# The last stage of a four-layer kernel, its operations issued in a listed order in place of a greedy one

## The chip, the core and the metric

The kernel runs on one core of a Trainium2 chip. The metric is the device time of one execution in microseconds (us). Three runs of the kernel before gave 3882.3, 3878.21 and 3872.31 us, so its median is 3878.21 us. The core's engines are called PE (matrix multiply; PEld is its weight load), DVE (vector), ACT (scalar and activation), POOL (GpSimd) and SP (it issues most of the DMA transfers). Each of them works through its own list of instructions, and a semaphore holds an instruction back until what it reads has been written.

## The reference, cut to what matters

The reference takes an image of 4 samples, 56 x 56 pixels, 128 channels, and passes it through four layers, each with a residual: window attention, a graph layer, a Fourier neural operator with attention, and a convolution. The changed code is the last stage: the end of the third layer and the whole of the fourth. This is what it has to compute:

```python
attention = _inorm(projd + xa, norm_g[1], norm_b[1])
an = _inorm(attention, norm_g[2], norm_b[2])
m = _fno_layer(an, wM0, wM0s, bM0s, (H, W), (norm_g[3], norm_b[3]), act=True)
m = _fno_layer(m, wM1, wM1s, bM1s, (H, W), (norm_g[4], norm_b[4]), act=False)
output = _inorm(m, norm_g[5], norm_b[5]) + attention
# ... x = x + output; then the fourth layer on the group norm of x:
y = lax.conv_general_dilated(xc, W, window_strides=(1, 1), padding=[(pad_t, pad_t), (0, 0)], ...) + b
agent_sum = jnp.sum(y, axis=3, keepdims=True)
time_sum = jnp.sum(y, axis=2, keepdims=True)
g = (agent_sum + time_sum - y) / scale
out = jax.nn.relu(g + res)
```

`_fno_layer` is a Fourier transform cut to a few frequencies, a weighting of these, and the transform back, plus a skip connection. In the kernel, transforms are matmuls with constant matrices, and every `_inorm` needs a sum over the whole image before anything after it can go on. The fourth layer needs the group norm's sums over a whole sample.

## The kernel before, where the change and the prediction touch it

The last stage is written as a plan of 788 operations. Each has an engine, a cost in the plan's own model, what it comes after, and which buffers it takes and gives back. The plan is issued by a greedy rule: of all operations that may go, the one that could start first in the model goes next, ties in the order of the plan.

```python
class Plan:
    HOP, SETS = 0.25, 1.3
    # ...
    def issue(self):
        free, table, left = {}, None, list(self.ops)
        # ...
        while left:
            best = None
            for op in left:
                if any(a.end is None for a in op.after):
                    continue
                t = max([free.get(op.engine, 0.0)] + [a.end + a.lag + self.HOP * (a.engine != op.engine)
                                                      for a in op.after])
                # ... buffers that have to come free
                if t is not None and (best is None or t < best[0] - 1e-9):
                    best = t, op
            # ...
            op.run()
            free[op.engine] = op.end = t + op.cost
```

One half of a sample (28 of its 56 rows) goes through `half_sample`. The halves are called 0a, 0b, 1a ... 3b in this document. This is the chain of one half, cut to the operations that come up later; `op(engine, cost, after)` adds an operation, and the work of an operation is on the lines under it.

```python
h = over_h("y", "h", [put_dc], d, v)              # PE  h1: transform along one axis
c = over_c("c", k.gw, [plain], ds, v)             # PE  c1: mix of channels
# ... adds (DVE), squares (ACT)
w1, z1, z = over_w("att", adds)                   # PE  w1, then a copy on ACT
var = sums("s1", k.ones_px, "sq", HH, sqs, [sq])  # PE  s1, then a reduction on DVE
total, square, t1 = weighted(w.M0, [z1], z, y)    # PE  two products, DVE two, POOL total, ACT square
factors = everywhere("r", 2, [inverses], ...)     # PE  F1, then copies on DVE
var = sums("f", k.ones[:112], "t1", 32, [square], [t1])     # PE  f
# POOL skip (2.8), POOL normed (2.8)
h = over_h("y", "h", [total, under], d, v)        # PE  h2
sc = scaled("h", "f", w.g123, [h, inv], d, y)     # DVE
c = over_c("c", k.gv, [sc], ds, v)                # PE  c2, then adds2 (DVE), gelus (ACT)
w2, z2, z = over_w("g", gelus)                    # PE  w2
total, square, t1 = weighted(w.M1, [z2], z, y, "dc")        # PE  p2, ... POOL total, ACT square
var = sums("q", k.ones[:112], "t1", 32, [square], [t1])     # PE  q
h = over_h("y", "h", [total, var], d, v)          # PE  h3
sc = scaled("h", "q", w.ng[:, 4:5], [h, inv], d, y)         # DVE
@op("POOL", 0.9, [sc, spread_copy])
def less_mean():
    nc.gpsimd.tensor_add(V.v[:, :, :HH], V.v[:, :, :HH], bc(V.dcs, 2, HH))
c = over_c("c", k.gv, [less_mean], ds, v)         # PE  c3
for i in range(2):                                # DVE adds3, ACT squares
    # ...
var = sums("r5", k.ones_px, "sq", HH, sqs, [sq])  # PE  r5
factors = everywhere("r5x", 1, [view], ...)       # PE  F5
for i in range(2):
    p = plan.add("POOL", 1.5, last, [factors])
    p = plan.add("POOL", 1.8, sum2, [p, sum1], (), [a] if i else [])
    whole.done.append(plan.add("DVE", 1.1, stats, [p]))
@op("DVE", 1.77, whole.done[-2:])
def sums_a(): ...
@op("DVE", 3.0, whole.done[-2:])
def sums_l(): ...
```

After both halves, `last_layer` does the fourth layer of a sample. Its operations are called L0 to L3 here.

```python
@op("DVE", 0.3, whole.done)
def aggregate(): ...
@op("PE", 0.3, [aggregate], [b1])
def means(): ...
# deviations (DVE), variances (PE), root (ACT), scale (DVE)
@op("PE", 1.5, [variances] + whole.sums, [b3])
def over_l(): ...
# offsets (DVE), over_taps (PE), rows (DVE)
for i, (j, n) in enumerate(pieces):               # four pieces of 16, 16, 16 and 8 rows
    p1 = plan.add("POOL", n / 10, spread, [rows], [o])
    p2 = plan.add("PE", 0.3 * n, convolve, [scale] + whole.done, [d])
    p = plan.add("DVE", 0.06 * n, add, [p1, p2], (), [d])
    p = plan.add("ACT", 0.055 * n, relu, [p])
    plan.add("POOL", 0.115 * n, store, [p], (), [o, ("x", b)], lag=3.0)
```

The stage begins with eight turns (transposes on PE) that bring the attended rows out of a big buffer: four for samples 0 and 1 (`R0`), four for samples 2 and 3 (`R1`). That buffer's place is taken by the residual images `o_x`, whose loads therefore wait for the last turn; `constant` (ACT) and then `sum1` (POOL) are the first to use them.

## Time and profile before

The page of the profile covers one execution of 3873.3 us. The stage in question is its last tenth: the first turn starts at 3471.46 us, the last matmul ends at 3867.2 us.

| part of the span | us |
|---|---|
| whole span | 3873.3 |
| first matmul of the last stage to its last matmul | 395.7 |
| from the last matmul to the end | 6.1 |
| PE busy over the whole span | 3546.0 |
| POOL busy over the whole span | 1210.6 |

How to read what follows: a line of a timeline gives start, duration, engine, line of the kernel, instruction, tiles written and read, and in square brackets how long the engine sat idle before it and what released it. The chain of waits names for each engine and line what it waited for, with the total, the number of times and the longest. The half-sample names are not in the trace; they follow from the order in which the program's instructions stand on each engine, since every engine executes its list in that order.

## The change

The greedy rule is taken out, and `issue` gets a list of all 788 operation numbers. It goes through the list and only asserts that everything an operation comes after has been issued, and that the buffers it takes are free by then. The operations themselves, their buffers and their dependencies are as before. The list was searched for in the plan's model; it is for a shorter stage than the greedy order gives.

```diff
-    HOP, SETS = 0.25, 1.3
...
-    def issue(self):
-        free, table, left = {}, None, list(self.ops)
-        # ... the greedy rule shown above
-        return max(op.end for op in self.ops)
+    def issue(self, order):
+        assert sorted(order) == list(range(len(self.ops)))
+        users, taken = {}, {n: [] for n in self.buffers}
+        for op in self.ops:
+            for g in op.gives:
+                users[g] = users.get(g, 0) + 1
+        for n in order:
+            op = self.ops[n]
+            assert all(a.end for a in op.after)
+            for b, key in op.takes:
+                taken[b].append(key)
+                old = len(taken[b]) - 1 - self.buffers[b]
+                assert old < 0 or not users[b, taken[b][old]]
             op.run()
+            op.end = True
             for g in op.gives:
                 users[g] -= 1
...
+OUTPUT_ORDER = """
+0 40 119 227 306 10 3 2 1 4 5 13 12 11 14 15 6 9 7 8 18 19 16 17 41 228 120 42 307 121 43 45 44 122 124 229 47
+... 19 more lines ...
+781 782 785 786 787
+"""
...
-        plan.issue()
+        plan.issue([int(n) for n in OUTPUT_ORDER.split()])
```

The two orders, engine by engine, at the places that the prediction speaks of (read from the instructions of the two built programs; an apostrophe marks the second of two equal operations of a half):

```
PE, start
 before: R0 turns x4, 0a.h1 0b.h1 0a.c1 1a.h1 1b.h1 0a.w1, R1 turns x4, 0a.s1 0a.p1 0a.p1' 0b.c1 0a.F1 ...
 after:  R0 turns x4, 0a.h1 0b.h1 0a.c1 1a.h1 0a.w1 0b.c1 0a.s1 0a.p1' 0a.p1 0b.w1 0b.s1 0a.F1 0b.p1 0a.f
         0b.F1 0b.p1' 0a.h2 1a.c1 1b.h1 0b.f 0a.c2 1a.s1 0b.h2, R1 turns x4, 0a.w2 0b.c2 0a.p2' 0a.p2 1a.w1 ...
POOL, middle
 before: ... 2a.last 2a.sum2 2a.last' 2a.sum2' 2b.total' 3a.clear' 3a.sum1 3b.clear 2b.less_mean ...
 after:  ... 3a.skip L1.spread x3 3a.normed 3a.clear' 2b.total' 3a.sum1 2a.less_mean 3b.total 2b.less_mean
         3b.skip 3b.normed 3b.sum1 3a.total' 2a.last' 3b.clear' 2b.last' ...
DVE, end of sample 0
 before: ... 0b.stats' 0b.sums_a 0b.sums_l L0.aggregate 2a.add L0.deviations ...
 after:  ... 0b.stats' L0.aggregate 0b.sums_l 0b.sums_a L0.deviations ...
PE, tail
 before: L1.convolve L2.means 3a.q L1.convolve x3 L2.variances L2.over_l 3a.h3 3b.w2 L2.over_taps 3a.c3 3b.p2 3b.p2'
         3a.r5 3a.F5 3b.spread 3b.q 3b.h3 3b.c3 3b.r5 3b.F5 L2.convolve x4 L3.means L3.variances L3.over_l
         L3.convolve L3.over_taps L3.convolve x3
 after:  L1.convolve 3b.c2 3a.q L1.convolve x2 3b.w2 L1.convolve 3b.p2' L2.means 3b.p2 L2.variances L2.over_l
         3a.h3 3b.spread L2.over_taps 3b.q 3a.c3 3b.h3 3a.r5 3b.c3 3a.F5 3b.r5 3b.F5 L2.convolve x3 L3.means
         L2.convolve L3.variances L3.over_l L3.convolve L3.over_taps L3.convolve x3
POOL, tail
 before: 3b.total' 3a.last 3a.sum2 3a.last' 3a.sum2' 3b.less_mean 3b.last ...
 after:  3b.total' 3a.less_mean L2.spread x3 3b.less_mean 3a.last' 3a.last 3a.sum2' 3a.sum2 3b.last' ...
DVE, tail
 before: 3a.stats 3b.scaled 3a.stats' 3a.sums_a 3a.sums_l 3b.adds3 3b.adds3' 3b.reduce ...
 after:  3a.adds3 3a.adds3' 3b.scaled 3a.reduce ... 3b.adds3 3a.copies 3b.adds3' 3b.reduce ... 3a.stats' 3b.copies ...
```

## The prediction

> **What bounds the kernel now.** I read the page first, for where the span goes, and then only the last stage: its timeline on PE, the chain of waits on PE, and the timelines of POOL and DVE just ahead of each long wait. The page says that PE is busy almost everywhere, so an order can only win what PE idles or what it does slowly:

> ```profile
> span 3873.3 us, 79430 instructions
> PE   6899999989998998999989989999998989989988
> PEclk8999999999999999999999999999998989998888
> ```

> Each digit is the share, in tenths, of a slice of 96.8 us. In the last four slices, where the stage lies (3471.5 to 3867.2 us, 395.7 us), PE is at 8 to 9 tenths, and its granted clock is lower than in most of the kernel. The stretches of the stage show both:

> ```profile
> 3471.00:3500.00 29.00, 24.13 (x188) 20.21 (x188) 10.11 (x20) 14.76 (x32) 0.28 (x2) 0.94 0.39 143
> 3540.00:3556.00 16.00, 16.00 (x82) 13.52 (x83) 1.92 (x5) 4.34 (x5) 7.61 (x4) 0.57 0.00 0
> 3600.00:3620.00 20.00, 17.61 (x91) 11.39 (x91) 12.81 (x27) 5.75 (x7) 1.28 (x1) 0.66 0.06 24
> 3727.00:3754.00 27.00, 20.47 (x118) 14.24 (x110) 14.62 (x21) 9.42 (x11) 10.76 (x8) 0.62 0.00 1
> 3804.00:3832.00 28.00, 17.88 (x79) 10.15 (x80) 13.10 (x22) 3.35 (x6) 14.14 (x10) 0.57 0.00 1
> ```

> Columns: stretch, length, busy us of PE, PEld, DVE, ACT, POOL, granted clock, DMA share, GB/s. In the last two PE idles 6.5 and 10.1 us and its clock is about 0.6. What ended the waits, longest first, by the chain of waits on PE:

> ```profile
> PE o_b L1967 <- ACT o_t L1956: 9.1, 4, 6.5
> PE o_d L1900 <- POOL o_v L2159: 6.3, 4, 3.6
> PE o_b L1967 <- ACT o_sq L2019: 3.9, 1, 3.9
> PE o_b L2241 <- DVE o_mv L2236: 2.8, 2, 2.1
> ```

> All waits on PE inside the stage add up to 38.1 us. The cause of the 6.5 us wait (2b.q) is seen on POOL: the total that 2b.q needs (L1952) starts only after two multiplies and two additions of another half (L2182, L2185).

> ```profile
> 3724.23 1.50 POOL L2182 TENSOR_TENSOR o_a<-o_a,o_f 128x784 f32<-128x784 f32 x1
> 3725.81 1.85 POOL L2185 TENSOR_TENSOR o_x<-o_x,o_a 128x784 f32<-128x784 f32 x1
> 3727.63 1.49 POOL L2182 TENSOR_TENSOR o_a<-o_a,o_f 128x784 f32<-128x784 f32 x1
> 3729.20 1.83 POOL L2185 TENSOR_TENSOR o_x<-o_x,o_a 128x784 f32<-128x784 f32 x1
> 3730.99 2.08 POOL L1952 TENSOR_TENSOR o_y<-o_t,o_t 112x896 f32<-112x896 f32 x1
> ```

> In the tail the same happens twice: 3b.less_mean (L2159, 0.84 us) stands behind the last and sum2 of 3a, and on DVE 3b.adds3 (L2166) behind 3a's sums:

> ```profile
> 3813.66 1.77 DVE L2196 TENSOR_REDUCE o_nl<-o_x 128x28 f32<-128x1568 f32 x1
> 3815.34 3.01 DVE L2200 TENSOR_REDUCE o_na<-o_x 128x56 f32<-128x1568 f32 x1
> 3818.26 2.22 DVE L2166 SCALAR_TENSOR_TENSOR o_a<-o_t,t_w_ms,o_d 128x392 f32<-128x392 f32 x4
> ```

> 3b.c3 had ended at 3816.5, so adds3 lost 1.8 us there, and PE stood for 3.91 us.

> [...] half-clock windows begin in or right after the gaps at 3604, 3652, 3727, 3768 and 3807 us, but those at 3652 and 3768 are of 1.4 and 1.7 us only, and the window at 3541 has no gap ahead, only over_w and other matmuls of few columns. So a removed gap is worth more than itself, but not every slow window goes with one.

> **The change part by part.** No operation is added or removed; 737 of the 788 stand at another place in the order of issue. First the sum of the stage. Taking for each kind of PE operation its fastest instance (w 3.09, h 1.57, c 1.44, product 1.5, a 16-row convolve 4.51, and so on, by the count in the plan) gives 286.5 us of PE work. The remaining 109.2 us of the 395.7 are 38.1 of waits, 51.4 lost in half-clock windows (half of PE's busy time in them), and 19.7 of small scatter. The last item stays.

> For the waits I compared, for every pair of PE operations joined through other engines, the PE work placed between them in each order with the shortest time between them that this trace shows. Where the filler is shorter, the rest is a wait.

> Waits that I expect to go:
> - 2b.q: 6.53. In the new order 2b.total' stands ahead of 2a's last and sum2 (6.7 us of POOL).
> - 3b.c3: 3.65, of which some 3.5 go, since less_mean no longer stands behind 3a's four operations and h3 to c3 needs only scaled (1.15) and less_mean (0.84).
> - 3b.r5: 3.91, of which 1.6 go. From c3 to r5 the shortest seen is 3.12, and 0.81 of filler (3a.F5) lies between.
> - means of L0 and what follows, 2.06 + 0.33: aggregate stands ahead of sums_l and sums_a (3.02 + 1.77). Means of L1 and what follows, 0.71 + 0.81 + 0.35: the filler from 1b.F5 to it is 20.4 us instead of 11.3, where 14.2 was the shortest seen.
> - the first product after w2, 1.54 (0a) and 1.05 (1a): no filler before, a c (1.44) now.
> - 3b.c2: 1.73, filler 0 before, 5.4 now.
> - c3 of 0b, 1b and 2a behind less_mean: 1.55 + 0.30 + 0.78.
> - 3a.F5 1.44, L3.variances 1.28, 2a.f 1.42: each has filler now.
> Sum: 6.5 + 3.5 + 1.6 + 2.4 + 1.9 + 2.6 + 1.7 + 2.6 + 4.1 = 26.9 us.

> Waits that the new order makes, by the same comparison: 0a.w1 0.9, 0b.F1 2.1 (s1 to F1 needs 5.06, filler 2.93), 1b.f 1.6, L1.over_taps 1.7, 2a.F1 1.35, 3a.w1 0.9, L2.over_taps 2.5 (needs 4.18, filler 1.69), 3a.r5 1.5. Sum 12.5. Net: 26.9 - 12.5 = 14.4 us less waiting, so about 24 us remain.

> The clock: of the windows lost, I take as gone the ones that the removed gaps set off: 3732 to 3753 (9 us lost), 3603 to 3616 (6.5), 3770 to 3773 (1.7), 17 in all. The tail's window (3807 to 3831, 7.5) I keep, since h3, c3, r5 and F5 of two halves are still alone there. The new waits will set off one or two others at the mean of 4.7 (51.4 over 11): minus 6. Net 11 us. The 6.1 us after the last matmul stay.

> The plain sum is 14.4 + 11 = 25 us. I take off 5 for queues that pairs of operations do not show (below), and predict 3878 - 20 = 3858 us.

> **The rivals.**
> (1) The order is good only in its model: where it has put operations next to each other to the tenth of a us, a real one that is late holds up its whole engine. Against it: the costs in the plan are near the measured ones (sums_l 3.0 and 3.05, last 1.5 and 1.50, skip 2.8 and 2.81), so the model sees the queues of POOL and DVE. For it: it knows nothing of the clock, and its PE times are full-speed ones. This would make about 3875.
> (2) A transfer takes the place: the R1 turns come at about 36 us of PE work instead of 14, so the residual images are loaded some 20 us later. Before, all three loads were issued at 3496.4 to 3497.7 and moved until 3510; constant began at 3512.0. Now constant stands on ACT only about 4.2 us after the last R1 turn (w2 3.1, its copy 0.9). If the first image lands alone, in a third of the 13 us, ACT waits 1 us and PE nothing. If all three land together, ACT waits 9 us and 1a's products some 4.6 us more. For the first: the loads are issued one after another on one queue. This would make 3863.
> (3) The clock gives all back: the same slow windows elsewhere, and only 14 us of waits gone: 3868. Or it gives more: with half of the 51 us gone, 3842.

> **Range and chances.** Rival 3 both ways spans 3842 to 3868, rival 1 adds up to 3875, and the three runs before differ by 10 us. So 3858, with 3838 to 3875 for 8 in 10. A change of 2% is 77.6 us, of the 109 that are not work at its fastest; 89.5 of those are waits and clock, so faster by more than 2% would need nearly all of them: 0.02. Slower by more than 2% would need three times the waits there are now: 0.01. Within 2%: 0.97.

> **What would show it right or wrong.** Right: no q waits over 2 us for its square on ACT; c3 no longer waits 3.6 us for POOL; the waits on PE in the stage sum to 20 to 28 us; the mean clock in the stage rises from 0.85 (the twelve stretches of the stage, weighted) to near 0.88; the stage's first to last matmul takes 370 to 380 us. Wrong: the waits sum to over 35, or ACT stands on the load of o_x for over 5 us, or the clock stays. The first 3471 us must be unchanged; if they move by more than 5 us, the comparison itself is blurred.

## The result and the profile after

The kernel with the listed order takes 3816.0 us (median of four runs; 3815.0 to 3821.9) against 3878.4 us before (four runs; 3872.3 to 3882.3): a ratio of 0.9844, with a 95% interval of 0.9827 to 0.9861. That is 62 us less where 20 were predicted, and outside the range given. The page of the profile after begins:

```profile
span 3813.2 us, 79448 instructions
...
PE   6899999989999898899999989998998889998998
...
PEclk8999999999999999999999999999998989999999
```

The slices are now 95.3 us long. PE is no busier by these digits in the last four than before; what has changed is the clock under them, from 8 to 9 tenths. The whole stage, first matmul to last, is one stretch in each trace. The columns are stretch, length, busy us (and instructions) of PE, PEld, DVE, ACT and POOL, then granted clock, DMA share and GB/s. Before:

```profile
3471.46:3867.20 395.74, 357.60 (x2232) 236.74 (x2232) 226.37 (x395) 146.17 (x206) 218.30 (x131) 0.85 0.12 47
```

After, the whole stage, then the start of 0a's second half, the surroundings of 2b.q, and the tail in two parts:

```profile
3467.39:3807.07 339.68, 322.20 (x2232) 210.91 (x2232) 225.68 (x395) 144.71 (x206) 218.55 (x132) 0.96 0.15 55
...
3510.00:3536.00 26.00, 22.86 (x151) 17.13 (x143) 11.78 (x22) 14.55 (x21) 5.21 (x6) 0.80 0.46 186
3688.00:3708.00 20.00, 20.00 (x174) 13.87 (x177) 11.24 (x22) 12.60 (x15) 14.17 (x11) 1.00 0.00 1
3745.00:3775.00 30.00, 25.50 (x168) 15.48 (x165) 21.47 (x47) 7.88 (x12) 20.47 (x14) 0.94 0.09 33
3775.00:3807.00 32.00, 31.14 (x105) 16.98 (x103) 20.02 (x32) 6.54 (x8) 22.89 (x14) 1.00 0.18 75
```

The same 2232 matmul instructions keep PE busy for 35.4 us less, because they run at 0.96 of the clock in place of 0.85; DVE and POOL do the same work in the same time. Taken by the sum that the prediction used, the stage is:

| part of the stage, us | before | after |
|---|---|---|
| work at its fastest | 286.5 | 286.5 |
| waits on PE | 38.1 | 17.0 |
| half of PE's busy time in half-clock windows | 51.4 | 11.9 |
| scatter | 19.7 | 24.3 |
| first to last matmul | 395.7 | 339.7 |

By this sum the 56.1 us come from the clock (39.5) and the waits (21.1), less 5 of scatter. The two spans differ by 60.1 us; the other 4 lie ahead of the stage, which began at 3467.4 us instead of 3471.5. Its start moved between 3467 and 3483 us over all the profiles of this study, with nothing changed ahead of it, so these 4 us are not the change's. The 6.1 us after the last matmul stayed.

The chain of waits on PE in the stage after, longest first (what waited, for what, total us, times, longest):

```profile
PE o_d L1863 <- ACT o_y L2014: 3.2, 1, 3.2
PE o_d L1894 <- ACT o_y L2342: 2.3, 1, 2.3
PE o_b L1947 <- ACT o_t L1936: 2.0, 2, 1.2
...
PE o_b L1947 <- ACT o_sq L1999: 1.5, 2, 1.2
...
PE o_d L1880 <- POOL o_v L2139: 0.9, 2, 0.5
```

Line numbers are 20 lower than before for the same statements: L1947 is L1967 before, L1880 is L1900. The waits of q and f for a square went from 9.1 us in four (longest 6.5) to 2.0 in two, the waits for less_mean from 6.3 to 0.9. The first line is 0a.h1 at the very start (2.9 before); the second, 0a.w2, is new and comes up again below. What became of the two inversions is seen on POOL after: the totals of 2b (L1932) and 3b's less_mean (L2139).

```profile
3696.57 2.10 POOL L1932 TENSOR_TENSOR o_y<-o_t,o_t 112x896 f32<-112x896 f32 x1 [2.55 <-DVE o_dc L1926]
...
3761.66 0.84 POOL L2139 TENSOR_TENSOR o_v<-o_v,o_dcs 128x392 f32<-128x392 f32 x1 [1.97 <-DVE o_v L1990]
```

Both now find POOL idle and are released by their own input: it is POOL that waits, 2.55 and 1.97 us, not the operation. On DVE in the tail it is the same:

```profile
3764.19 1.16 DVE L2146 SCALAR_TENSOR_TENSOR o_a<-o_t,t_w_ms,o_d 128x392 f32<-128x392 f32 x2 [0.92 <-PE o_d L1880]
...
3773.21 3.06 DVE L2180 TENSOR_REDUCE o_na<-o_x 128x56 f32<-128x1568 f32 x1
```

3b.adds3 (L2146) starts as 3b.c3 ends, and the sums of 3a (L2180), which stood ahead of it before, come 9 us later.

## Experiments

By the sum above, most of the difference is clock. So there were two theories. The theory of waits: the half clock follows from PE standing still for other engines, and what counts is the chain through them. The theory of the clock: half clock is a cost by itself, set off by what PE is given to do, wait or no wait. Each kernel below was run beside the kernel before on the same chip, and its ratio is to that. Its loss at half clock and waits are those of its profiled execution.

**Is it the order at all?** The greedy order written out as a list:

```diff
-OUTPUT_ORDER = the searched list
+OUTPUT_ORDER = the list that the greedy rule gives
```

> The greedy order written out as a list: the same instructions in the same order as before. Both theories that follow (windows: PE's clock is halved for a 3.41 us window and more after a window in which PE streams too few columns, whether by a wait or by matmuls of few columns; waits alone: the clock windows fall where they fall and a removed wait is worth only itself) expect the time of before within 5 us, the waits on PE in the stage near 38 us and the half-clock windows at the same places, some 51 us lost in them. A third theory, that the windows are luck of phase, expects them at other places and a loss that differs from 51 by over 10 us.

Measured: 3877.0 us, ratio 1.001 (0.9998 to 1.0022); stage 392.2 us, waits 41.0, loss at half clock 43.3. So the list itself costs and brings nothing. The loss at half clock differs by 8 us from that of the kernel before although the operations and their order are the same (the stretch at 182 to 203 us of the stage is missing): differences of that size between two profiles mean nothing here.

**Fill the waits of the tail and of 2b.q**, with the greedy order kept: matmuls of a constant matrix of 448 columns, into a bank that the next operation overwrites, placed directly before the operation that waits.

```diff
 PE (greedy order)
-... 2b.q ... 3a.F5 ... 3b.q ... 3b.c3 ... 3b.r5 ... 3b.F5 ...
+... 7x const 2b.q ... 2x const 3a.F5 ... const 3b.q ... 4x const 3b.c3 ... 4x const 3b.r5 ... const 3b.F5 ...
```

> The greedy order, with matmuls of constants put into PE's longest waits (7 before 2b.q, 2 before 3a.F5, 1, 4, 4 and 1 before 3b.q, c3, r5, F5; 0.78 us each); their results are overwritten. No wait of the other engines goes. Windows theory: the half-clock windows at 3732 to 3753 and 3807 to 3831 us go, 9 + 7.5 us: 12 to 18 us faster. Waits alone: no faster, or slower by 1 to 5 us where the filling runs on past the wait.

Measured: 3869.2 us, ratio 0.9994 (0.9983 to 1.0006); loss at half clock 45.0. The 24 us at half clock in the tail shrank to 3.4. The tail on PE (constants are L1847):

```profile
3816.84 3.19 PE L1847 MATMUL o_d<-slot,t_shared 128*128 128x448 f32 x8
3821.47 1.60 PE L1889 MATMUL o_d<-o_v,t_images 32*128 32x392 f32 x16 [1.44 <-POOL o_v L2150]
3823.00 3.27 PE L1847 MATMUL o_b<-slot,t_shared 128*128 128x448 f32 x8
3828.40 2.51 PE L1957 MATMUL o_b<-o_sq,c_ones_px 128*32 128x392 f32 x8 [2.13 <-ACT o_sq L2010]
```

3b.c3 (L1889) takes 1.60 us at full clock where it took 3.00, and still waits after the constants. From the end of 3a.F5 to the first L2.convolve it is 19.7 us, against 20.5 before. So in a stretch where PE waits for a chain of others, the half clock is nearly free. This speaks for the theory of waits, and the 12 to 18 us that the other theory gave were missed: half-clock windows came up elsewhere (213 to 240 us of the stage, 271 to 285).

**Mend single inversions by hand.** In the tail, in the middle, and all three that the prediction named:

```diff
 tail
 POOL
-3b.total' 3a.last 3a.sum2 3a.last' 3a.sum2' 3b.less_mean 3b.last
+3b.total' 3b.less_mean 3a.last 3a.sum2 3a.last' 3a.sum2' 3b.last
 DVE  3a.stats, stats' moved behind 3b.view, 3a.sums_a, sums_l behind 3b.copies'
 middle
 POOL
-3a.normed 2a.last 2a.sum2 2a.last' 2a.sum2' 2b.total' 3a.clear' 3a.sum1 3b.clear
+3a.normed 2b.total' 2a.last 2a.sum2 2a.last' 2a.sum2' 3a.clear' 3a.sum1 3b.clear
 DVE  2a.stats, stats' moved behind 3a.adds2', 2a.sums_a, sums_l behind 2b.adds3'
 all three: tail, middle, and
 DVE  L0.aggregate before 0b.sums_a, 0b.sums_l; L1.aggregate before 1b.sums_a, 1b.sums_l
```

> The greedy order, but in the tail 3b.less_mean ahead of 3a's last and sum2 on POOL, and 3b.adds3 to the root ahead of 3a's stats and sums on DVE. Waits alone: c3 3.65 to about 0.5, r5 3.91 to 2.3, so 5 us faster. Windows theory: the same and up to 7.5 us of clock besides, 8 to 13 us faster.

> The greedy order, but 2b.total' ahead of 2a's last and sum2 on POOL, and 2a's stats and sums behind 2b.scaled and adds3 on DVE. Waits alone: the wait of 6.53 us at 2b.q goes, 5 to 7 us faster. Windows theory: the window of 20.5 us after it goes too (9 us), 13 to 17 us faster.

> The greedy order with the three inversions mended that the prediction named: 2b.total' ahead of 2a's last and sum2, 3b.less_mean and adds3 ahead of 3a's, aggregate of samples 0 and 1 ahead of sums_a and sums_l. If these inversions are what the searched order gains by: the sum of their waits, 16 us, and as much of the clock, 25 to 35 us faster. If a removed wait only hands over to the next one in the chain, as it did at 2b.q: 8 to 14 us faster.

Measured: tail 3872.8 us, ratio 1.000 (0.9989 to 1.001); middle 3867.1, 0.9983 (0.9975 to 0.9991); all three 3867.0, 0.9977 (0.9968 to 0.9985). The tail's version gained nothing that can be told from noise, where both theories gave 5 us or more. In the middle's, the wait of 2b.q fell from 6.53 to 1.53 us as meant, but PE's timeline in the middle shows where it went, 3b.w1 (L1894):

```profile
3735.38 0.59 PE L1947 MATMUL o_b<-o_t,c_ones 112*32 112x224 f32 x8 [1.53 <-ACT o_t L1936]
...
3743.35 2.00 PE L1894 MATMUL o_d<-t_images,o_t 128*128 128x64 f32 x12 [3.29 <-POOL o_t L1853]
```

And on POOL:

```profile
3739.57 3.50 POOL L2114 TENSOR_TENSOR o_x<-o_x,o_t 128x1568 f32<-128x1568 f32 x1
3743.00 0.29 POOL L1853 MEMSET o_t<- 128x224 f32 x1
```

3b.clear (L1853), 0.29 us, which w1 needs, stands as before behind the four operations of 2a and 3a.sum1 (3.50 us); now that q is earlier, PE gets to w1 before them. The waits in all fell only from 38.1 to 37.5 us here and to 35.8 in the tail's version, and with all three they were 38.5, no less than before. Here an inversion mended alone handed its wait on to the next operation that the queue held back.

**Half of the list.** The searched order for the first 300 operations and the greedy one for the rest (74 of 192 operations on PE), and the greedy one for the first 394 with the searched one for the rest:

```diff
+first: searched[:300] + [n for n in greedy if n not in searched[:300]]
+second: greedy[:394] + [n for n in searched if n not in greedy[:394]]
```

> The first 300 operations of the searched list (to 1a.h3, the 74th of PE's 192 operations), then the rest in the greedy order. If the gain is made place by place, as the lag of the stage against its work grew (10 us by there), 6 to 12 us faster than before. If it takes the whole list, no faster than 3 us.

> The first 394 operations in the greedy order (to 1b.c3, the 98th operation of PE), then the rest in the searched order. If the gain is made place by place: 35 to 45 us faster (56 us of the stage less some 15 gained by there). If it takes the whole list: under 25 us.

Measured: first 3878.9 us, ratio 1.0006 (0.9994 to 1.0017); second 3836.1, 0.9892 (0.9866 to 0.9918). The first part alone brings nothing, and it had little to bring: PE ended its 74th operation at 125.8 us of the stage here, at 125.4 with the whole list and at 127.3 before, with about as much work behind it. The second alone brings 39 of the 62 us: waits 22.8, loss at half clock 30.7. The first result was the mark set for a gain that takes the whole list, the second the mark for one made place by place. Most of the gain is made in the second part; where the other 23 us come from when both stand together, these two runs don't show.

**A half-clock stretch without a wait.** The prediction had noticed the window at 3541 us, where nothing waits. Two stretches of the kernel before show it:

```profile
3537.81:3541.22 3.41, 3.41 (x39) 3.39 (x38) 1.58 (x4) 0.62 (x2) 2.12 (x2) 1.00 0.00 0
...
3541.22:3554.90 13.68, 13.68 (x65) 11.80 (x66) 1.75 (x4) 4.34 (x5) 6.06 (x3) 0.50 0.00 0
```

In the first, PE is busy for all of its 3.41 us at full clock, and the next 13.68 us run at half. What is special in the first is in what PE does: a spread (7 columns), 1a.F1 (14 columns) and 1b.w1 (64 columns), one after the other. So only 1a.F1 was moved, ahead of two products of 448 columns, to leave w1 alone with its few columns:

```diff
 PE (greedy order)
-0b.c2 1a.p1 1a.p1' 0a.spread 1a.F1 1b.w1
+0b.c2 1a.F1 1a.p1 1a.p1' 0a.spread 1b.w1
```

> The greedy order with one operation of PE moved: 1a.F1 (matmuls of 14 columns) ahead of 1a's two products (448 columns) and not behind them, so that 1b.w1 (64 columns) follows the products. No wait stands here in either order. Windows theory: the half-clock window of 13.6 us at 70 to 83 us of the stage, seen in all five traces of the greedy order so far, goes without a wait being removed: 5 to 7 us faster in the stage up to 3a's start. Waits alone: nothing changes, within 2 us.

Measured: 3872.0 us, ratio 0.9989 (0.9979 to 0.9998). The same place on PE, before and with the move (the line is that of w1 and w2, here 0b.w2). Before:

```profile
3543.82 6.24 PE L1914 MATMUL o_d<-t_images,o_t 128*128 128x64 f32 x28
```

With the move:

```profile
3546.90 3.34 PE L1894 MATMUL o_d<-t_images,o_t 128*128 128x64 f32 x28
```

The stretch is gone, no wait having been removed, and PE is 6.3 us ahead at the operation after it, 0b.p2. At the end only some 3 are left (3.3 by the medians, where one theory gave 5 to 7 and the other under 2): new half-clock windows came at 90 to 97 us of the stage, and others shifted. The profiles can't confirm these 3 us: the stage took 392.2 us here, and as long with the listed greedy order, which has nothing moved. That is the second thing that single changes run into.

**The price at equal PE time.** The searched order, and before 2b.s1 either 17 matmuls of 7 columns or 5 of 448, which take PE about as long:

```diff
 PE (searched order)
-2b.w1 2b.s1 1b.F5 2a.w2
+2b.w1 17x const(7 columns) 2b.s1 1b.F5 2a.w2     # poor
+2b.w1 5x const(448 columns) 2b.s1 1b.F5 2a.w2    # rich
```

> The searched order with 17 extra matmuls of constants of 7 columns ahead of 2b.s1, some 3.8 us of PE's time, results overwritten. Its twin has the same time in matmuls of 448 columns. Windows theory: PE is busy but streams next to nothing, so a window of half clock follows: 3.8 us and 4 to 10 us of clock, 8 to 14 us slower than 3816. Waits alone (PE busy is PE busy): 4 us slower, like the twin.

> The searched order with 5 extra matmuls of constants of 448 columns ahead of 2b.s1, some 3.9 us of PE's time. Both theories: no half-clock window follows, about 4 us slower than 3816. The difference to the twin is the price of one half-clock window alone, since both hold PE for the same time and take no wait away.

Measured: poor 3839.8 us, ratio 0.9917 (0.9893 to 0.9941); rich 3818.7, 0.9861 (0.984 to 0.9883). PE in the poor one, with the constants at L1848 and 2a.w2 at L1905:

```profile
3651.33 4.22 PE L1848 MATMUL o_b<-slot,t_shared 128*128 128x7 f32 x34
...
3658.68 6.21 PE L1905 MATMUL o_d<-t_images,o_t 128*128 128x64 f32 x28
```

In the rich one:

```profile
3646.18 3.98 PE L1848 MATMUL o_b<-slot,t_shared 128*128 128x448 f32 x10
...
3651.80 3.32 PE L1905 MATMUL o_d<-t_images,o_t 128*128 128x64 f32 x28
```

And the 30.67 us from the first constant on, poor first, then rich:

```profile
3651.33:3682.00 30.67, 30.30 (x191) 22.17 (x193) 18.49 (x24) 9.62 (x15) 22.80 (x12) 0.78 0.16 53
```

```profile
3646.18:3676.85 30.67, 30.03 (x212) 19.80 (x215) 23.90 (x34) 12.37 (x22) 27.41 (x15) 1.00 0.17 53
```

PE is busy in both (30.30 and 30.03), but at 0.78 of the clock in one. The constants differ by 0.24 us and the medians by 21 us. In the two profiled executions the stages differ by 4.9 us only (347.2 and 342.3); the profiled one was the fastest of the poor kernel's, the others went up to 3847 us. So where PE is the bound, 4 us of few columns, with no wait added, cost 4.9 us of the stage in the one execution that was traced and 21 us by the medians. What the slower executions lost besides was not traced.

**One wait that the list left.** 0a.w2 waits 2.34 us after. ACT just ahead of it:

```profile
3511.95 0.95 ACT L2085 ACTIVATE o_t<-o_a,factors 128x784 f32<-128x784 f32 x1
3512.90 1.28 ACT L2051 ACT_TABLE_LOAD   x1
...
3516.46 1.28 ACT L2085 ACT_TABLE_LOAD   x1
3517.76 0.95 ACT L2085 ACTIVATE o_t<-o_a,factors 128x784 f32<-128x784 f32 x1
```

Between 0a.gelu and 0a.gelu' (L2085) the list puts 1a's roots (L2051) and the copies of two turns, so the table is loaded twice more, 1.28 us each. What w2 then waits for by the trace (L2342) are copies of the last turns, which stand behind 0a.gelu' on ACT. One operation was moved, so that the two gelus share one load:

```diff
 ACT (searched order)
-0a.gelu 1a.roots R1.copy_rows R1.copy_rows 0a.gelu' R1.copy_rows
+0a.gelu 0a.gelu' 1a.roots R1.copy_rows R1.copy_rows R1.copy_rows
```

> The searched order with one operation moved on ACT: 0a.gelu' directly behind 0a.gelu, so that the root of 1a no longer stands between them and two loads of the activation table (1.28 us each) go. Waits alone: the wait of 2.34 us at 0a.w2 goes or halves, 1 to 3 us faster than the searched order's 3816. Windows theory: the half-clock window of 10 us after it goes too, 5 to 8 us faster, about 3809 to 3811.

Measured: 3807.6 us, ratio 0.9832 (0.9811 to 0.9853). ACT and PE at that place now:

```profile
3511.63 1.79 ACT L2085 ACTIVATE o_t<-o_a,factors 128x784 f32<-128x784 f32 x2
```

```profile
3518.67 3.34 PE L1894 MATMUL o_d<-t_images,o_t 128*128 128x64 f32 x28 [0.68 <-ACT o_y L2342]
```

The same operation in the kernel with the listed order:

```profile
3519.93 6.04 PE L1894 MATMUL o_d<-t_images,o_t 128*128 128x64 f32 x28 [2.34 <-ACT o_y L2342]
```

The stage has 17 table loads in place of 19. The wait of w2 fell from 2.34 to 0.68, and w2 itself from 6.04 to 3.34 us, because the half-clock stretch from 53 to 63 us of the stage was gone; the loss at half clock is 3.4 us, 8.5 less. The waits of the stage in all did not fall (17.9 us against 17.0): one of the last turns now waits 1.52 us just ahead of w2. So what was won is clock. To see it without the scatter between chips, the searched order and this one were run again side by side, and constants were put into the waits that are left:

> The searched order once more, to stand beside the next run on the same chip: 3816 us within 6.

> The searched order with the second gelu of 0a directly behind the first on ACT. If the two table loads between them cost what the earlier run showed: 7 to 10 us less than the searched order beside it, with the window at 53 to 63 us of the stage gone. If that was the scatter of runs: within 3 us of it.

> As the run before, and besides matmuls of constants of 448 columns in the remaining waits that set off half-clock windows: 3 ahead of 0a.h1, 1 ahead of 1b.f, 1 each ahead of 3b.r5 and 3b.F5. Windows theory: the windows at the start (1.7 us lost), after 1b.f (3.4) and in the tail (1) go too: 3 to 6 us faster than the run before. Waits alone: no gain, up to 2 us slower.

Measured: side by side 3821.4 us (3819.7 to 3824.9) for the searched order and 3812.9 (3811.5 to 3816.9) with the one operation moved, 8.5 us less; ratios 0.9862 (0.9844 to 0.9879) and 0.984 (0.9823 to 0.9857). This time the half-clock stretch at 53 us shrank from 10.2 to 6.8 us; the expectation had it gone. Waits were the same in both (18.2 and 18.0 us), and the loss at half clock fell from 11.9 to 6.8. The constants (before 0a.h1, 1b.f, 3b.r5 and 3b.F5 in that version) gave 3812.6 us, 0.9844 (0.9823 to 0.9864), beside 3807.6 without them on the same chip, and a stage of 332.68 us against 332.67: they won nothing, where the theory of the clock gave 3 to 6 us. The loss at half clock stayed at 3.4 us, one window having gone at the start and one come in the tail.

**The clock alone, over the whole stage.** The greedy order with 1a.F1 moved as above, and constants in every wait of over 0.7 us that can take them (forty, not the forty-two of the text below):

```diff
 PE (greedy order, 1a.F1 moved), constants of 448 columns before
+0a.h1 3, 0a.p2 2, 0a.F5 1, 0b.c3 2, 1a.p2 2, 2a.f 2, 2b.q 7, 3b.c2 2, 3a.F5 2, 3b.q 1, 3b.c3 4, 3b.r5 4, 3b.F5 1
+L0.means 3, L1.means 1, L1.variances 1, L3.variances 2
```

> The greedy order with 1a.F1 moved ahead of 1a's products, and 42 matmuls of constants placed directly before the operations that wait (17 places), which take away none of the chains of other engines. If the clock is a cost of its own: the loss in half-clock windows falls from some 45 us to under 20 and the time by 20 to 35 us, to 3840 to 3858. If the half clock mostly lies where PE waits for a chain anyway: the loss falls too, but the time by less than 12 us, to 3865 or more, since the waits come back as longer idle stretches or as the constants' own time.

Measured: 3849.1 us, ratio 0.9931 (0.9911 to 0.9951), beside 3821.4 for the searched order on the same chip. The stage is:

```profile
3482.99:3853.15 370.16, 353.29 (x2312) 225.61 (x2312) 228.25 (x395) 146.40 (x206) 218.56 (x131) 0.97 0.13 51
```

and in the run of the searched order beside it:

```profile
3476.09:3817.00 340.91, 322.36 (x2232) 210.50 (x2232) 225.34 (x395) 144.71 (x206) 218.59 (x132) 0.96 0.15 55
```

This cuts the gain in two. The loss at half clock is the same in both, 11.9 us. In the greedy order PE still stands still or fills, and for longer than it stood before: forty constants of about 0.8 us (five took 3.98) are 32 us, and with the 16.5 of waits left that is 48, against 38.1 before. So from 395.7 to 370.2 us, 25.6 us, is the clock with no wait of another engine taken away, and from 370.2 to 340.9 us, 29.3 us, is the order with the clock kept. The medians on this chip (3874.2 us before, 3849.1, 3821.4) give 25.1 and 27.7. The theory of the clock gave 20 to 35 us and the other one under 12: the first holds. But the loss fell by 39.5 us for 25.6 of time. Of the other 14, some 10 went into this longer stand, and 4 into scatter. Time at half clock that had been hidden in waits, as in the tail above, would come back so, and so would constants that outlast their wait; this run does not tell the two apart. The cut is good to a few us only, also because the moved F1 is worth some 3 us by itself.

## Why the prediction was wrong

**What bounds the kernel.** Right: the gain is in PE's waits and its clock, and nowhere else.

**The waits to go**, 26.9 us. Nearly all went: 2b.q and L0's means are under 0.3 us, 3b.c3 is 0.47 (3.65 before), 3b.r5 is 1.52, where 2.3 had been left to it. Summed over the same places, 26.8 us went. Right in kind, and in size.

**The new waits**, 12.5 us in eight places. Those eight measured 3.3: 0b.F1, 2a.F1 and 3a.r5 under 0.25 each, 0a.w1 0.32, 1b.f 0.85, L1.over_taps 0.56, 3a.w1 0.38, L2.over_taps 1.05. The step that failed was to take the shortest time that the trace before showed between two operations of PE as the time that they need. After, s1 to F1 takes 3.13 us (taken as 5.06), c3 to r5 2.19 (3.12), over_l to over_taps 2.83 (4.18). These are the places where the three shortest times had been seen, 0b.F1, 3a.r5 and L1.over_taps before:

```profile
3514.78 1.06 PE L1994 MATMUL o_b<-o_r,slot 128*128 128x14 f32 x8
3802.01 0.93 PE L1967 MATMUL o_b<-o_sq,c_ones_px 128*32 128x392 f32 x8
3695.66 0.85 PE L2295 MATMUL o_b<-o_nlp,t_w_W 128*128 128x56 f32 x6
```

None has a bracket: PE had not waited there, it came straight from other work. So these times were PE's own work in between, and only showed that the chain through the other engines needs no longer. On the other side, 0a.w2 (2.34) and 2a.q (1.18) were not foreseen: the pairs have no place for a table load on ACT (0a.w2) or for a total that stands behind a sum1 of 3.5 us on POOL (2a.q). The waits that remain are 17.0 us, not 24.

**The clock**, net 11 us. This is the step that made the prediction wrong: it took half-clock windows for what follows a gap on PE, an estimate that its trace bore out in part only: gaps of 1.4 and 1.7 us, or none at all, stood ahead of some of them. It took as gone only the windows that followed a removed gap (17 us), kept the tail's "since h3, c3, r5 and F5 of two halves are still alone there", and added 6 for new ones. The loss fell by 39.5. Of the eleven half-clock stretches of before, with 34 windows in all, four with 7 windows are left, and the tail's 24 us are 3.4. The runs showed half-clock stretches that come and go with no gap: the one at 3541 us went with one F1 moved, and 4.22 us of matmuls of 7 columns, with no wait added, were followed by a w of 6.21 us where it took 3.32 after matmuls of 448. What the windows ahead of half clock mostly share is that few columns stream in them, whether PE waits or works (87 of 91 under a share of 0.40, last section). The prediction had the instance before it, the window at 3541 us, and did not count with it. Its reading of the gaps was thin as well: of the five that it names, 2b.q's is 6.53 us, but the one at 3604 is 2.06 us, and ahead of the stretch at 3807 stand waits of 1.44 and 0.86, the 3.65 coming inside it. As time by itself, with the other engines' chains kept, the clock is worth 25.6 us: more than twice the 11.

**The allowance of 5 us** for queues that pairs don't show is not seen as a wait: the waits came out 7 us under the 24 that the sum without it gave, and 24.3 us of scatter against 19.7 is all that could be set to it.

**The rivals.** (1), the order good only in its model, falls: waits of 17.0 us in place of 38.1. (2), the later loads of o_x: they were issued at 3517.6 us and constant began at 3526.8, with no wait for them on PE. In the version with the gelu moved, ACT waited 1.3 us for a load; PE did not wait behind it. (3) named the right thing, a clock that gives more, and was still short: it set half of 51 us gone, 3842 us, where 77% went.

**The marks set.** No q waits over 2 us: right. c3 no longer waits: right. Waits of 20 to 28 us: 17.0. Clock near 0.88: 0.96. Stage of 370 to 380 us: 339.7. The first 3471 us within 5: 4.1 less, right.

## What to carry to other kernels

In a stage like this one, where the matmul engine is busy 90% of the time and its granted clock is below full (0.85 here), go through it in windows of 3.41 us, the shortest stretch of one clock in the traces here, and ask how many columns stream in each, not how long PE is idle: keeping the clock up was worth about as much here as the order's shorter waits (25.6 and 29.3 us). Don't judge a reordering by mending one wait at a time: three mended inversions gave 8 us, the whole list 62; the wait went to the next in the queue, and half clock came up elsewhere. And before trusting a shortest time seen between two operations as what they need, ask whether the engine waited there at all: where it did not, the need can be shorter, as it was by 1 to 2 us in three pairs here.

## What the runs showed of the hardware

| clock in the window | share in which columns stream | next window has the other clock | of these, before and after |
|---|---|---|---|
| full | under 0.35 | 58 of 58 | 7 of 7 |
| full | 0.35 to 0.40 | 29 of 45 | 7 of 8 |
| full | 0.40 to 0.45 | 2 of 39 | 0 of 8 |
| full | 0.45 and more | 2 of 904 | 1 of 150 |
| half | under 0.75 | 0 of 133 | 0 of 21 |
| half | 0.75 to 0.85 | 15 of 33 | 3 of 6 |
| half | 0.85 and more | 76 of 84 | 12 of 14 |

The five traces with constants, which had no part in this, agree: under 0.35, 14 of 15 are followed by half clock, at 0.45 and more none of 426; at half clock under 0.75 none of 27 is followed by full clock, at 0.85 and more 19 of 21. How long PE is idle sorts the windows worse: of 105 windows of the twelve traces at full clock in which PE was busy for less than 0.7, 41 were followed by full clock, and 9 of the 91 losses came after windows busy for over 0.9.

So in these twelve traces 87 of the 103 full-clock windows with a share under 0.40 were followed by half clock, and none of the 133 half-clock windows under 0.75 by full clock. The 28 instructions of a w are an instance of the second: 28 x 64 columns at twice 0.84 ns are 3.0 us in the 6.24 that 0b.w2 takes at half clock, a share of 0.48. Before, 10 full-clock windows of the stage were under 0.40 and 34 were at half clock; after, 5 and 7. The window at 3537.8 us has no gap on PE, and its share is 0.365. These are counts: what makes the clock change was not shown. And the shares are bound to this stage's matmuls in fp32; other types and tile sizes were not tried.

Where the windows fall on the work differs from execution to execution: the first change to half clock came at 32.35 us of the span before and at 31.75 after, in a part that the change leaves as it is. The times differ too: the same greedy order lost 51.4 us in one profile and 43.3 in another, and the kernel with 7-column constants took 3827 to 3847 us. That the place of the windows makes this scatter fits, but no run held it fixed.
